# Layer 2 scan steps of two channel-and-state groups over half a chunk, with two PSUM places for the scan's inputs and two products ahead of two scans

One core of one Trainium2 chip. The metric is the device time of the whole program, in microseconds (us), of the slowest (here the only) core.

## The reference

Four layers on a 2 x 64 x 96 x 96 image: attention, a Mamba block, a bidirectional Mamba over rows and then columns, and a depthwise filter. The change touches layer 2. Cut to what matters there:

```python
def step(h, inp):                      # one position t of one sequence
    dt_t, B_t, C_t, x_t = inp
    dA = jnp.exp(dt_t[:, :, None] * A)                       # the decay
    h = dA * h + dt_t[:, :, None] * B_t[:, None, :] * x_t[:, :, None]
    return (h, jnp.einsum('nds,ns->nd', h, C_t))
...
y = jnp.swapaxes(ys, 0, 1) + x * p['Dp']
y = y * jax.nn.silu(z)
```

Sequences are 96 long and start from zero in layer 2. Layer 1 has the same step, but one sequence of 9216 per image, so there the state is carried from chunk to chunk.

## The kernel before

A unit is one chunk of 768 positions (8 sequences) in one direction. The 128 channels times 16 states are 2048 rows, taken as 16 groups of 128, one group a step: partition p holds state p // 8, and in step n channel (p + 8n) mod 128. (The prediction calls them channel groups.) For each step a read brings 128 rows of `dt` and `dt*x`, from row 8n on, from a copy in DRAM that holds every row twice; ScalarE turns `dt` into decays, VectorE (DVE) multiplies `dt*x` by `B` into PSUM and scans, GpSimd (POOL) multiplies by `C`, and TensorE (PE) gathers: it puts every row back to its channel and adds it into `y`, so that after 16 steps the states are summed.

```python
def read(self, u, step):
    u.dtu[step] = self.work("spread", 2 * CH, bufs=7)
    self.nc.sync.dma_start(out=u.dtu[step], in_=u.rows[8 * step : 8 * step + P])

def decay(self, u, step):
    da = u.dtu[step][:, :CH]
    self.nc.scalar.activation(da, da, AF.Exp, scale=u.w.rates[:, step : step + 1])

def scan(self, u, step):
    da, x = u.dtu[step][:, :CH], u.dtu[step][:, CH:]
    _, bx = self.two(self.ps_x, "x", "bx")          # one PSUM place, 2 x 512 columns
    nc.vector.tensor_mul(bx, x, u.B)                # u.B: 2 x 512 columns
    h = u.h[step] = self.work("h", bufs=7)
    ...
    nc.vector.tensor_tensor_scan(h[:, way], da[:, way], bx[:, way], first, ALU.mult, ALU.add)
    ...
    nc.gpsimd.tensor_mul(h, h, u.C)

def gather(self, u, step):                          # two matmuls, halves of the chunk
    ...
    self.nc.tensor.matmul(p, lhsT=self.t.gather[step], rhs=u.h[step][:, bass.ts(j, HALF)], ...)

# per unit, at fixed steps: (offset from the unit's first step, piece)
PIECES = (... (-25, "gate_mm"), (-23, "gate_read"),        # ScalarE: copy, table load, Silu, table load
          (-21, "step_mm"), (-19, "step_read"), (-18, "step_exp"), (-17, "step_kept"), ...
          (-9, "step_u"), (-8, "step_write"),              # GpSimd makes the rows, SyncE writes them
          (18, "y_read"), ...)                             # ScalarE drains y from PSUM
```

In the timelines shown here each engine's instructions stand in program order. That order for a step is: read of step n+5, decay of step n+3, product and scan of step n, gather of step n-2, then the pieces of that step.

## Time and profile before

| | before |
|---|---|
| time, median (range) of the 3 runs known then | 8538.82 us (8531.84 to 8540.03) |
| layer 1, first scan to first scan of layer 2 | 1188 us, 384 steps |
| layer 2, first 384 steps | 1170 us, 3.05 us each |
| layer 2, other 1152 steps (the quiet part) | 3346 us, 2.91 us each |

The stretches are taken from the starts of the scans in the trace. In the first part of layer 2 the weights of later blocks are still prepared between the steps. The lines on which the argument rests are in the prediction, with how to read them.

### The profile page before, as it was taken

The numbers are of one execution on the slowest core, as the hardware profiler recorded it, in microseconds if no ns is written. First come the engines' busy times: TensorE is split into PE (matmuls) and PEld (weight loads), VectorE is DVE, ScalarE is ACT, GpSimd is POOL, SyncE is SP. The second block draws the span as 40 slices with busy tenths as digits, with TensorE's granted clock in tenths as the row PEclk, the third lists the DMA queues.
The fourth block names the chain that finished last, engine by engine and source line by source line (L and its number), as shares of the span: only waits on it lengthen the run. The fifth ranks groups of instructions, "written<-read, shape, count | busy, mean of one in ns | idle before, by whom it ended". The sixth has DMA issues, their size and how long they took to land.

```text
span 8543.3 us, 77007 instructions
## 1 busy us (share of the span) xinstructions
PE 7689.6 (90%) x24578; PEld 3325.3 (39%) x24578; DVE 7074.4 (83%) x5136; ACT 4738.5 (55%) x4817; POOL 4786.7 (56%) x3146
## 2 busy tenths in 40 slices
PE   9999999999998999998898888888888888888887
PEld 3333333333333444444444444444444444444443
DVE  6666666666664999988888999999999999999998
ACT  4444444444444665665556566665655655565562
POOL 0000000000001888888777888888888888888884
PEclk9999999999997998888889999999999999999999
DMA  1000000000002877777777888888888888888884
GB/s 40 1 1 1 1 1 1 4 4 4 4 4 80 299 288 278 295 277 281 283 289 284 292 312 304 305 310 299 310 305 303 308 297 310 301 305 305 300 313 182
DMA packets 317287, 1725.61 MB, mean 202 GB/s; under 512 B 35268, under 2 KB 36420, under 8 KB 316360
## 3 DMA queue, kind: packets, MB, share of 16 engines
q1 hardware_dynamic: 315424, 1717.56, 54.7%
q8 instruction: 195, 3.19, 0.2%
q10 hardware_dynamic: 1448, 3.05, 0.1%
q14 instruction: 220, 1.80, 0.1%
HBM read 1522.68 MB, written 197.79 MB: 201 GB/s over the span
## 4 chain that ended last, share of the span: by engine, by line
DVE 33%; POOL 11%; PE 8%; DMA 8%; issue 5%; ACT 3%; DVEq 1%; SPq 0%; POOLq 0%; ACTq 0%
DVE h L842 21%; DVE bx L838 11%; POOL h L845 8%; DMA spread<-rows 6%; PE y_ssm L854 3%; PE mm L661 2%; DMA rows<-dtu 2%; PE conv L745 1%; ACT spread L826 1%; PE B L832 1%; POOL dtu L802 1%; POOL state L844 1%; PE conv L739 1%; DVE xa L1167 1%; DVEq L842 1%
## 5 line engine op out<-in xcount | busy, mean ns | idle before, releaser
L845 POOL TENSOR_TENSOR h<-h,C 128x768 f32<-128x768 f32 x1920 | 3484.1, 1815 | 818.2 <-DVE h L842 767.0
L854 PE MATMUL y_ssm<-h,pair 128*128 128x384 f32 x7680 | 2958.7, 522 | 324.9 <-POOL h L845 322.3
L842 DVE TENSOR_TENSOR_SCAN h<-spread,bx 128x768 f32<-128x768 f32 x1536 | 2694.4, 1754 | 228.5 <-ACT spread L826 20.4
L854 PEld LDWEIGHTS y_ssm<-h,pair 128*128 128x128 f32 x7680 | 1445.9, 198 | 1748.7 <-POOL h L845 670.2
L838 DVE TENSOR_TENSOR bx<-spread,B 128x768 f32<-128x768 f32 x1920 | 1846.5, 962 | 239.0 <-PE B L832 172.6
L363 DVE TENSOR_TENSOR acc_e<-acc_e,e 128x1536 f32<-128x1536 f32 x792 | 1390.0, 1755 | 684.4 <-ACT e L307 645.2
L826 ACT ACTIVATE spread<-spread,xa 128x768 f32<-128x768 f32 x1536 | 1405.1, 930 | 989.1 <-DMA spread<-rows 956.4
L307 ACT ACTIVATE e<-f_exp 128x1536 f32<-128x1536 f32 x864 | 1207.1, 1449 | 1223.7 <-PE f_exp L297 1223.7
L336 POOL TENSOR_TENSOR xa<-xa,t_att 64x512 f32<-64x512 f32 x36 | 45.5, 1263 | 2612.7 <-ACT t_att L334 2612.7
L314 PE MATMUL y_att<-e,xb 128*64 128x512 f32 x5184 | 1243.6, 601 | 0.0
L297 PE MATMUL f_exp<-theta,phi 64*128 64x512 f32 x5184 | 1234.4, 606 | 1.0 <-DVE xb L280 0.5
L297 PEld LDWEIGHTS f_exp<-theta,phi 64*128 64x128 f32 x5184 | 466.2, 186 | 754.6 <-issue 460.8
L842 DVE TENSOR_TENSOR_SCAN h<-spread,state,bx 128x768 f32<-128x768 f32 x384 | 696.0, 1813 | 66.9 <-ACT spread L826 15.7
L314 PEld LDWEIGHTS y_att<-e,xb 128*64 128x64 f32 x5184 | 341.5, 136 | 830.7 <-issue 829.3
L745 PE MATMUL conv<-xn,xa 64*128 64x384 f32 (+3 forms) x1536 | 595.5, 531 | 51.4 <-DVE xa L589 19.5
L756 ACT ACTIVATE raw<-conv,cols 128x768 f32<-128x768 f32 x120 | 108.2, 901 | 878.6 <-PE conv L745 632.6
L826 ACT ACTIVATE spread<-spread,rates 128x768 f32<-128x768 f32 x384 | 351.0, 930 | 148.6 <-DMA spread<-rows 146.1
L745 PEld LDWEIGHTS conv<-xn,xa 64*128 64x128 f32 x1536 | 291.8, 200 | 341.9 <-issue 139.0
L661 PE MATMUL mm<-raw,xa 128*128 128x384 f32 x768 | 287.4, 497 | 65.7 <-ACT xb L893 64.7
L832 PE MATMUL B<-raw,xa 128*128 128x384 f32 x384 | 181.2, 603 | 171.4 <-DVE bx L838 171.4
L792 POOL TENSOR_TENSOR kept<-dtu,kept 128x768 f32<-128x768 f32 x120 | 218.3, 1820 | 64.4 <-ACT kept L785 64.3
L739 PE MATMUL conv<-xn,taps 64*128 64x384 f32 x384 | 193.5, 662 | 37.8 <-DVE xa L589 18.9
(200 smaller groups left out, 5530.5 us busy)
## 6 DMA issues: line engine op xcount, KB each, us to landing
spread<-rows SPq DMA_DIRECT2D x1920, 768.0 KB, 5.3
rows<-dtu SPq DMA_DIRECT2D x240, 768.0 KB, 5.8
image<-pre SPq DMA_DIRECT2D x11, 384.0 KB, 2.3
xb<-image SPq DMA_DIRECT2D x11, 384.0 KB, 7.1
xa<-in_x SPq DMA_DIRECT2D x1, 2304.0 KB, 21.5
out<-xa ACTq DMA_DIRECT2D x7, 240.0 KB, 2.0
out<-xa SPq DMA_DIRECT2D x1, 1200.0 KB
xa<-in_x SPq DMA_DIRECT2D x3, 384.0 KB, 11.5
```

What stands on the lines that cost most here:

```text
L297: nc.tensor.matmul(fs[j // 3][:, bass.ts(j % 3, NB)], lhsT=phi[at, bass.ts(m // 2, P)], rhs=theta[at, bass.ts(i, NB)], start=True, stop=True,)
L307: nc.scalar.activation(e, f, AF.Exp)
L314: nc.tensor.matmul(y[rows_of(m % 2)], lhsT=g[:, m, :], rhs=es[j // 3][:, bass.ts(j % 3, NB)], start=m < 2, stop=m >= KEYS - 2,)
L363: nc.vector.tensor_add(acc, acc, e)
L661: self.nc.tensor.matmul(o, lhsT=lhsT, rhs=x, start=n == 0, stop=n == len(terms) - 1)
L739: self.nc.tensor.matmul(p, lhsT=lhsT, rhs=x[:, c0 - j : c0 + HALF - j], **flags)
L745: self.nc.tensor.matmul(p3[:, :, o], lhsT=lhsT, rhs=x3[:, :, i], **flags)
L826: self.nc.scalar.activation(da, da, AF.Exp, scale=u.w.rates[:, step : step + 1])
L838: nc.vector.tensor_mul(bx, x, u.B)
L842: nc.vector.tensor_tensor_scan(h[:, way], da[:, way], bx[:, way], first, ALU.mult, ALU.add)
L845: nc.gpsimd.tensor_mul(h, h, u.C)
L854: self.nc.tensor.matmul(p, lhsT=self.t.gather[step], rhs=u.h[step][:, bass.ts(j, HALF)], start=False, stop=step == self.STEPS - 1,)
```

## The change

Its intent: VectorE should not wait for its own last instruction. The scan depended on the product just ahead of it, and the next product had to write the PSUM place that the scan had just read. With a second place, and the order product, product, scan, scan, neither is so. To make room for the second place `B` and `y` shrink: in layer 2 a step becomes two groups over half a chunk (still 768 columns), with `B` and `y` of half a chunk in a tile of NB = 512 columns each. Both kernels allocate 8 x 512 columns of PSUM in these layers; that no more would fit was the premise. Decays go straight into the tile in which the scan runs in place. The core of the diff (layer 1's branch and set-up cut):

```diff
+        self.places = [self.wide(ps.tile([P, 2 * NB], FP, name=f"place{i}")) for i in range(2)]
+        self.low = [ps.tile([P, NB], FP, name=f"low{i}")[:, :HALF] for i in range(2)]
...
     def read(self, u, step):
-        u.dtu[step] = self.work("spread", 2 * CH, bufs=7)
-        self.nc.sync.dma_start(out=u.dtu[step], in_=u.rows[8 * step : 8 * step + P])
+        u.dtu[step] = self.work("spread", 2 * CH, bufs=6)
+        half, groups = self.paired(step)
+        for q, n in enumerate(groups):
+            row = u.rows[8 * n : 8 * n + P, bass.ts(half, CH)]
+            self.nc.sync.dma_start(out=u.dtu[step][:, bass.ts(q, CH)], in_=row)
     def decay(self, u, step):
-        da = u.dtu[step][:, :CH]
-        self.nc.scalar.activation(da, da, AF.Exp, scale=u.w.rates[:, step : step + 1])
+        h = u.h[step] = self.work("h", bufs=9)
+        for q, n in enumerate(self.paired(step)[1]):
+            dt = u.dtu[step][:, q * CH : q * CH + HALF]
+            self.nc.scalar.activation(h[:, bass.ts(q, HALF)], dt, AF.Exp, scale=u.w.rates[:, n : n + 1])
+    def inputs(self, u, step):
+        bx = self.places[step % 2][1].rearrange("p (q t) -> p q t", q=2)
+        x = u.dtu[step].rearrange("p (q a t) -> p q a t", q=2, a=2)[:, :, 1]
+        B = self.low[0].unsqueeze(1).to_broadcast([P, 2, HALF])
+        self.nc.vector.tensor_mul(bx, x, B)
     def scan(self, u, step):
+        bx = self.places[step % 2][1]
+        nc.vector.tensor_tensor_scan(h[:, way], h[:, way], bx[:, way], 0.0, ALU.mult, ALU.add)
+        C = u.C[:, bass.ts(self.paired(step)[0], HALF)]
+        nc.gpsimd.tensor_mul(h, h, C.unsqueeze(1).to_broadcast([P, 2, HALF]))
+    def y_half(self, u):                    # new piece at step 10: first half of y out of its tile
+        u.y = self.work("yg")
+        self.nc.scalar.copy(u.y[:, :HALF], self.low[1])
...  # in the loop over steps s of a unit
-                self.scan(*at(n))
-            if s == self.STEPS - 1 and at(n + 1):
-                self.shared(at(n + 1)[0])
+                elif s % 2 == 0:
+                    self.inputs(u, s)
+                    self.inputs(u, s + 1)
+                self.scan(u, s)
+                if u.paired and s == 6:
+                    self.shared(u, 1)       # B of the second half
+                if s == (14 if u.paired else 15) and unit(n // self.STEPS + 1):
+                    self.shared(after)      # B of the next unit's first half
```

More of the change, by code (lines that the diff above doesn't have):

```diff
@@ L630, with __init__ @@
     DECAY = 3
-    def __init__(self, k, tables, wk, dram, ps_b, ps_x, ps_y, ps_m):
+    def __init__(self, k, tables, wk, dram, ps, ps_m):
         self.k, self.nc, self.t = k, k.nc, tables
-        self.wk, self.dram, self.ps_b, self.ps_x, self.ps_y, self.ps_m = wk, dram, ps_b, ps_x, ps_y, ps_m
+        self.wk, self.dram, self.ps_m = wk, dram, ps_m
+        self.places = [self.wide(ps.tile([P, 2 * NB], FP, name=f"place{i}")) for i in range(2)]
+        self.low = [ps.tile([P, NB], FP, name=f"low{i}")[:, :HALF] for i in range(2)]
     def work(self, tag, n=CH, **kw):
@@ L639, in two, with wide @@
     @staticmethod
-    def two(pool, tag, name):
-        p = pool.tile([P, 2 * NB], FP, tag=tag, name=name)
+    def wide(p):
         return [p[:, NB - HALF : NB], p[:, NB : NB + HALF]], p[:, NB - HALF : NB + HALF]
@@ L650, in open @@
     def open(self, name="mm"):
-        return self.two(self.ps_m, "m", name)
+        return self.wide(self.ps_m.tile([P, 2 * NB], FP, tag="m", name=name))
     def half(self, sides, j, terms, rows=slice(0, P)):
@@ L671, in halves, with by_half @@
         return lambda j: t[:, bass.ts(j, HALF)]
+    @staticmethod
+    def by_half(t):
+        return t.rearrange("p (j t) -> p j t", j=2)
     def norm_centre(self, u):
@@ L775, in step_read @@
         u.both = self.work("dtu", 2 * CH, bufs=1)
-        u.dt, u.e = u.both[:, :CH], u.both[:, CH:]
-        u.kept = self.work("kept", bufs=1)
-        nc.scalar.activation(u.e, u.p, AF.Abs, bias=u.w.dt_b)
-        nc.scalar.activation(u.dt, u.p, AF.Relu, bias=u.w.dt_b)
+        order = "p (j a t) -> p a j t" if u.paired else "p (a j t) -> p a j t"
+        both = u.both.rearrange(order, a=2, j=2)
+        u.dt, u.e = both[:, 0], both[:, 1]
+        u.kept = self.by_half(self.work("kept", bufs=1))
+        p = self.by_half(u.p)
+        nc.scalar.activation(u.e, p, AF.Abs, bias=u.w.dt_b)
+        nc.scalar.activation(u.dt, p, AF.Relu, bias=u.w.dt_b)
     def step_exp(self, u):
@@ L787, in step_log @@
     def step_log(self, u):
-        u.log = self.work("log", bufs=1)
+        u.log = self.by_half(self.work("log", bufs=1))
         self.nc.scalar.activation(u.log, u.e, AF.Ln, bias=1.0)
@@ L801, in step_u @@
         nc = self.nc
-        nc.gpsimd.tensor_mul(u.e, u.dt, u.xc)
+        nc.gpsimd.tensor_mul(u.e, u.dt, self.by_half(u.xc))
         if not u.carry:
             first = W - 1 if u.rev else 0
-            nc.gpsimd.memset(u.dt.rearrange("p (n t) -> p n t", t=W)[:, :, first : first + 1], 1e30)
+            nc.gpsimd.memset(u.dt.rearrange("p j (n t) -> p j n t", t=W)[:, :, :, first : first + 1], 1e30)
     def step_write(self, u):
@@ L818, in c_read, with paired @@
         self.nc.scalar.copy(u.C, u.p)
+    def paired(self, step):
+        half, m = divmod(step, self.STEPS // 2)
+        return half, (2 * m, 2 * m + 1)
     def read(self, u, step):
-        u.dtu[step] = self.work("spread", 2 * CH, bufs=7)
-        self.nc.sync.dma_start(out=u.dtu[step], in_=u.rows[8 * step : 8 * step + P])
-    def decay(self, u, step):
-        da = u.dtu[step][:, :CH]
-        self.nc.scalar.activation(da, da, AF.Exp, scale=u.w.rates[:, step : step + 1])
-    def shared(self, u):
-        sides, u.B = self.two(self.ps_b, "b", "B")
-        for j, p in enumerate(sides):
-            self.nc.tensor.matmul(p, lhsT=u.w.bc[0], rhs=u.xc[:, bass.ts(j, HALF)], start=True, stop=True)
+        u.dtu[step] = self.work("spread", 2 * CH, bufs=6)
+        if not u.paired:
+            self.nc.sync.dma_start(out=u.dtu[step], in_=u.rows[8 * step : 8 * step + P])
+            return
+        half, groups = self.paired(step)
+        for q, n in enumerate(groups):
+            row = u.rows[8 * n : 8 * n + P, bass.ts(half, CH)]
+            self.nc.sync.dma_start(out=u.dtu[step][:, bass.ts(q, CH)], in_=row)
@@ new lines, in decay, with shared @@
+    def decay(self, u, step):
+        h = u.h[step] = self.work("h", bufs=9)
+        if not u.paired:
+            self.nc.scalar.activation(h, u.dtu[step][:, :CH], AF.Exp, scale=u.w.rates[:, step : step + 1])
+            return
+        for q, n in enumerate(self.paired(step)[1]):
+            dt = u.dtu[step][:, q * CH : q * CH + HALF]
+            self.nc.scalar.activation(h[:, bass.ts(q, HALF)], dt, AF.Exp, scale=u.w.rates[:, n : n + 1])
+    def shared(self, u, half=0):
+        if u.paired:
+            sides, halves = [self.low[0]], [half]
+        else:
+            (sides, u.B), halves = self.places[1], range(2)
+        for j, p in zip(halves, sides):
+            self.nc.tensor.matmul(p, lhsT=u.w.bc[0], rhs=u.xc[:, bass.ts(j, HALF)], start=True, stop=True)
@@ L834, in scan @@
+    def inputs(self, u, step):
+        if not u.paired:
+            u.bx = self.places[0][1]
+            self.nc.vector.tensor_mul(u.bx, u.dtu[step][:, CH:], u.B)
+            return
+        bx = self.places[step % 2][1].rearrange("p (q t) -> p q t", q=2)
+        x = u.dtu[step].rearrange("p (q a t) -> p q a t", q=2, a=2)[:, :, 1]
+        B = self.low[0].unsqueeze(1).to_broadcast([P, 2, HALF])
+        self.nc.vector.tensor_mul(bx, x, B)
     def scan(self, u, step):
         nc = self.nc
-        da, x = u.dtu[step][:, :CH], u.dtu[step][:, CH:]
@@ L837, in scan @@
-        _, bx = self.two(self.ps_x, "x", "bx")
-        nc.vector.tensor_mul(bx, x, u.B)
-        h = u.h[step] = self.work("h", bufs=7)
-        way = slice(None, None, -1) if u.rev else slice(None)
-        first = u.carry[:, step : step + 1] if u.carry else 0.0
-        nc.vector.tensor_tensor_scan(h[:, way], da[:, way], bx[:, way], first, ALU.mult, ALU.add)
-        if u.carry:
-            nc.gpsimd.tensor_copy(first, h[:, CH - 1 :])
-        nc.gpsimd.tensor_mul(h, h, u.C)
-    def gather(self, u, step):
-        if step == 0:
-            u.y_sides, u.y_all = self.two(self.ps_y, "y", "y_ssm")
-            for j, p in enumerate(u.y_sides):
-                self.nc.tensor.matmul(p, lhsT=u.w.direct, rhs=u.xc[:, bass.ts(j, HALF)], start=True, stop=False)
-        for j, p in enumerate(u.y_sides):
-            self.nc.tensor.matmul(
-                p,
-                lhsT=self.t.gather[step],
-                rhs=u.h[step][:, bass.ts(j, HALF)],
-                start=False,
-                stop=step == self.STEPS - 1,
-            )
@@ L862, in y_read @@
-    def y_read(self, u):
-        u.y = self.work("yg")
-        self.nc.scalar.copy(u.y, u.y_all)
+        h = u.h[step]
+        if not u.paired:
+            first = u.carry[:, step : step + 1]
+            nc.vector.tensor_tensor_scan(h, h, u.bx, first, ALU.mult, ALU.add)
+            nc.gpsimd.tensor_copy(first, h[:, CH - 1 :])
+            nc.gpsimd.tensor_mul(h, h, u.C)
+            return
+        bx = self.places[step % 2][1]
+        way = slice(None, None, -1) if u.rev else slice(None)
@@ new lines, in scan @@
+        nc.vector.tensor_tensor_scan(h[:, way], h[:, way], bx[:, way], 0.0, ALU.mult, ALU.add)
+        h = h.rearrange("p (q t) -> p q t", q=2)
+        C = u.C[:, bass.ts(self.paired(step)[0], HALF)]
+        nc.gpsimd.tensor_mul(h, h, C.unsqueeze(1).to_broadcast([P, 2, HALF]))
+    def gather(self, u, step):
+        if u.paired:
+            half, groups = self.paired(step)
+            parts = [(half, self.low[1], q, n) for q, n in enumerate(groups)]
+            begin, end = step % 8 == 0, step % 8 == 7
+        else:
+            parts = [(j, p, j, step) for j, p in enumerate(self.low)]
+            begin, end = step == 0, step == self.STEPS - 1
+        h = u.h[step]
+        if begin:
+            for half, p in {half: p for half, p, _, _ in parts}.items():
+                self.nc.tensor.matmul(p, lhsT=u.w.direct, rhs=u.xc[:, bass.ts(half, HALF)], start=True, stop=False)
+        for i, (_, p, q, n) in enumerate(parts):
+            stop = end and (i == 1 or not u.paired)
+            self.nc.tensor.matmul(p, lhsT=self.t.gather[n], rhs=h[:, bass.ts(q, HALF)], start=False, stop=stop)
@@ L866, in y_gate @@
+    def y_half(self, u):
+        if u.paired:
+            u.y = self.work("yg")
+            self.nc.scalar.copy(u.y[:, :HALF], self.low[1])
+    def y_read(self, u):
+        if u.paired:
+            self.nc.scalar.copy(u.y[:, HALF:], self.low[1])
+        elif not u.drained:
+            u.y = self.work("yg")
+            for j, p in enumerate(self.low):
+                self.nc.scalar.copy(u.y[:, bass.ts(j, HALF)], p)
     def y_gate(self, u):
@@ L920 @@
         (-8, "step_write"),
+        (10, "y_half"),
         (18, "y_read"),
@@ L927, with lates @@
     OTHER = (3, 5)
+    @staticmethod
+    def lates(now, s):
+        halves = now and now[0].paired
+        if s == 2 or (s == 10 and halves):
+            return ()
+        if s == 3 or (s == 11 and halves):
+            return (3, 2)
+        return (2,)
     def run(self, units, first, n_first, other):
         for u in units:
-            u.dtu, u.h = {}, {}
+            u.dtu, u.h, u.paired, u.drained = {}, {}, not u.carry, False
         steps = [(u, s) for u in units for s in range(self.STEPS)]
@@ L938, in run @@
         table = [[] for _ in range(self.STEPS)]
+        unit = lambda i: units[i] if i < len(units) else None
         for offset, name in self.PIECES:
@@ L961, in run @@
             if at(n):
-                self.scan(*at(n))
-            if s == self.STEPS - 1 and at(n + 1):
-                self.shared(at(n + 1)[0])
-            for late in {2: (), 3: (3, 2)}.get(s, (2,)):
-                if at(n - late):
+                u = at(n)[0]
+                if not u.paired:
+                    self.inputs(u, s)
+                elif s % 2 == 0:
+                    self.inputs(u, s)
+                    self.inputs(u, s + 1)
[3 more added lines that the diff above has]
+                if s == (14 if u.paired else 15) and unit(n // self.STEPS + 1):
+                    after = unit(n // self.STEPS + 1)
+                    if after.paired and not u.paired:
+                        for late in (2, 1, 0):
+                            self.gather(u, s - late)
+                        self.y_read(u)
+                        u.drained = True
+                    self.shared(after)
+            if n == -1:
+                self.shared(units[0])
+            for late in self.lates(at(n), s):
+                if at(n - late) and not (at(n - late)[0].drained):
                     self.gather(*at(n - late))
@@ L1002, in layers1_2 @@
         tc.tile_pool(name="ssm_d", bufs=2, space=bass.MemoryType.DRAM),
-        tc.tile_pool(name="ssm_b", bufs=1, space=PSUM),
         tc.tile_pool(name="ssm_x", bufs=1, space=PSUM),
-        tc.tile_pool(name="ssm_y", bufs=1, space=PSUM),
         tc.tile_pool(name="ssm_m", bufs=1, space=PSUM),
@@ L1018, in first @@
         def first(c):
-            ps, tag = ((m.ps_b, "b"), (m.ps_y, "y"), (m.ps_x, "x"))[c % 3]
-            pre.pointwise(k.xb[:, bass.ts(c, CH)], *m.two(ps, tag, "pc"))
+            pre.pointwise(k.xb[:, bass.ts(c, CH)], *(m.places[c % 3] if c % 3 < 2 else m.open()))
         carver = Carver(k.xa)
```

## The prediction

> **What bounds the kernel now.** I read the costliest groups of the page first, then the windows, then the chain of waits and the timeline of VectorE inside layer 2, then the list of waits. Layers 1 and 2 make 1920 scan steps, 384 in layer 1 and 1536 in layer 2. Each step is a product `bx` and a scan on VectorE (DVE), a product with `C` on GpSimd (POOL), one `Exp` on ScalarE (ACT), two gather matmuls (four instructions in the trace) and one 768 KB read.
>
> ```profile
> L845 POOL TENSOR_TENSOR h<-h,C 128x768 f32<-128x768 f32 x1920 | 3484.1, 1815 | 818.2 <-DVE h L842 767.0
> L842 DVE TENSOR_TENSOR_SCAN h<-spread,bx 128x768 f32<-128x768 f32 x1536 | 2694.4, 1754 | 228.5 <-ACT spread L826 20.4
> L838 DVE TENSOR_TENSOR bx<-spread,B 128x768 f32<-128x768 f32 x1920 | 1846.5, 962 | 239.0 <-PE B L832 172.6
> L826 ACT ACTIVATE spread<-spread,xa 128x768 f32<-128x768 f32 x1536 | 1405.1, 930 | 989.1 <-DMA spread<-rows 956.4
> ...
> 5600.00:6600.00 1000.00, 860.12 (x2319) 413.82 (x2318) 934.10 (x689) 612.58 (x674) 832.39 (x484) 0.97 0.83 306
> ```
>
> The reader is to see two things. DVE needs 1.754 + 0.962 = 2.716 us a step. In the quiet part of layer 2 (last line: busy PE, PEld, DVE, ACT, POOL, then clock, DMA share, GB/s) DVE is the busiest at 93%, and 345 scans begin there, 2.90 us a step. POOL waits mainly for the scan, ACT mainly for the DMA; neither sets the end. The chain says what the missing 7% is:
>
> ```profile
> 6004.37 0.97 DVE bx L838
> 6005.34 0.03 issue
> 6005.37 0.05 DVEq L842
> 6005.42 0.04 issue
> 6005.46 1.76 DVE h L842
> ```
>
> Product, 133 ns of nothing, scan, 34 ns (from the starts and ends in the trace), product. In the 133 ns the scan's semaphore wait is only answered when the product just before it has ended, and then the scan is issued. The median step is 2.883 us = 2.716 + 0.133 + 0.034. What DVE does when the next instruction is independent of the one in flight shows where weights of a later block are prepared between two steps:
>
> ```profile
> 4456.80 1.75 DVE L842 TENSOR_TENSOR_SCAN h<-spread,bx 128x768 f32<-128x768 f32 x1
> 4458.47 0.26 DVE L589 TENSOR_TENSOR xa<-mats,mm 128x128 f32<-128x128 f32 x1
> 4458.65 0.96 DVE L838 TENSOR_TENSOR bx<-spread,B 128x768 f32<-128x768 f32 x1
> 4459.74 1.75 DVE L842 TENSOR_TENSOR_SCAN h<-spread,bx 128x768 f32<-128x768 f32 x1
> ```
>
> 4456.80 + 1.75 is 4458.55, yet the next one starts at 4458.47; the product then starts at 4458.65, before 4458.73. In the trace such pairs overlap by 81 to 86 ns, in all 16 of the cases of this kind behind a scan, also where the second one waits for an older value of DVE's own semaphore.
>
> [...] 84 ns of overlap where nothing is waited for. [...] Product and scan have one input in PSUM; scans last 1753 to 1755 ns and POOL's products 1797 to 1830 ns in the window above[...]. [...] the trace has half-clock stretches of 3.4 us, two for each pair of units, where PE sits before `B`.
>
> **The change part by part.** In layer 2 a step becomes two channel groups over half the chunk, still 768 columns. The order of instructions on DVE is now product, product, scan, scan. Every one depends only on things at least two instructions back, so I expect all four joints of a pair of steps to overlap by 84 ns: (2 x 1.754 + 2 x 0.962 - 4 x 0.084) / 2 = **2.548 us** a step, against 2.883. That is 0.335 us x 1536 = 515 us if nothing else came to bind.
>
> Beside it, and not on DVE:
> - ACT makes two `Exp` of 384 columns instead of one of 768. From 830 ns for 768 and 1484 ns for 1536 columns a column costs 0.85 ns, so one of 384 is an estimated 0.60 us, two with ACT's own 0.1 us of overlap 1.1 us instead of 0.93. ACT goes from 28.1 to some 32 us a unit (16 steps).
> - Reads double in number at half the size. In the trace a 3072-byte packet took 121 ns (median) and a 6144-byte one 234, so the same bytes cost 3% more. The demand becomes 306 x 2.90 / 2.6 = 341 GB/s; over 12 us stretches the trace reached 424.
> - Decays go into the states' tiles (9 of them), so a read's buffer is free after the product and not after the scan; that pays for having 6 and not 7.
> - PE has as many matmuls as before, 108 a unit. At the 0.322 us between starts back to back this is 35 us, 38 us with the pauses at changes of weights. `B` is made twice a unit, and `y` is drained twice, with two more waits of PE.
> - Layer 1 keeps its dependent order: 384 steps, no change expected.
>
> **What binds instead.** A unit takes 46.6 us now. Floors after: DVE 16 x 2.548 = 40.8 us; POOL 38.7 us (its busy time without overlaps, per unit); PE about 38 us plus one or two waits of 2 us for a product before `B`; DMA 35 us (306 x 46.6 is 14.3 MB a unit, at 424 GB/s, and 3%). Nothing passes DVE, but POOL would be at 95% and PE at 93%, in queues in order, so some of the gain must come back as waits. The one I trust most:
>
> ```profile
> SPq L822 <- DVE h L842: 614.5, 257, 3.6
> SPq L811 <- POOL dtu L806: 141.0, 22, 6.7
> ...
> PEld B L832 <- DVE bx L838: 57.0, 22, 3.9
> PE B L832 <- DVE bx L838: 42.5, 22, 3.3
> ```
>
> The rows of the next unit are written when POOL has made them, once in each of 22 units, and SyncE stood 6.4 us for it. In one unit the write was issued 19.65 us before the next unit's first product, and that unit's first two reads landed 13.3 and 15.2 us after the write. At 2.55 us a step there are only some 16 us left. It should just fit; 2 us more of POOL's lag and each unit begins with a wait. I put 1.5 us a unit for all such waits: 42.3 us, **2.64 us** a step.
>
> The sum, from the starts of the scans: the last 1152 steps of layer 2 take 3346 us now (2.905 each) and 1152 x 2.64 = 3041 after: 305 saved. The first 384 take 1170 us (3.05 each), since weights are prepared between them and the clock is 0.81 to 0.93; PE is nearer its limit there, so I give half of the gain, 0.18 us x 384 = 69. 8539 - 374 = 8165, said as **8170 us**.
>
> **Rivals.**
> 1. Only the wait goes, not the overlap: joints of 34 ns as from scan to product now. Then 2.716 + 0.034 = 2.75 us a step, 0.133 less, at most 200 us: about 8340. For it: products wait on DVE's semaphore today and all show 34 ns. Against: there they wait for the instruction just ahead.
> 2. POOL becomes the bound. Its `h` times `C` now reads `C` twice through a repeated pattern of 2 x 384. A POOL product of 64 x 768 took 1.54 us flat and 1.81 us in 8 rows of 96, or 34 ns a row; two rows would add 0.03 to 0.07 us, 1 us a unit, still under DVE. At 0.2 us each POOL would need 42 us, 2.62 us a step plus waits: about 8230.
> 3. PE or the reads bind. With PE's clock at 0.85, as in the first part of layer 2, its 38 us become 43 to 45 us, 2.75 us a step: about 8330. Two small reads a step could also lower the DMA rate: the packets' own time is 0.83 of the engines' already, 40 us a unit with the 3%, and should they not gain by queueing, 330 GB/s is 2.69 us a step. Against: PE's idle times, which go with the half clock, should shrink.
> 4. The full 2.55 with hardly a wait: about 8050.
>
> **Range and chances.** I give the central course half, rival 1 and 3 together a quarter, rival 2 and 4 the rest: 8020 to 8340. Two per cent is 171 us, a step of about 2.79 us; rivals 1 and 3 together, or a new wait of 3 us at each unit, would be needed to miss it: faster 0.9, same 0.08, slower 0.02. A real slowdown needs the DMA to fall below 300 GB/s.
>
> **What would show it.** Right: scans still 1754 and products 962 ns, starts overlapping by 84 ns in the timeline, DVE above 95% busy, POOL near 92%, a median step near 2.55 and a mean near 2.64, layer 1 unchanged. Wrong: joints of 34 ns (rival 1); POOL's products above 1.95 us with DVE waiting on buffers (2); DVE waiting for `B`, or for `Exp` that wait for reads (3). The prediction fails most simply if the strided product or the scan in place is slower than 962 and 1754 ns: 0.1 us there costs 150 us.

## The result, and the profile after

| | before | after |
|---|---|---|
| time, median (range), 4 runs each | 8537.23 us (8531.84 to 8540.03) | 8177.18 us (8154.16 to 8195.08) |
| ratio of fast runs, 95% interval | | 0.9577 (0.9553 to 0.9602) |
| layer 1 | 1188 us | 1191 us |
| layer 2, first 384 steps | 1170 us, 3.05 each | 1071 us, 2.79 each |
| layer 2, other 1152 steps | 3346 us, 2.91 each | 3077 us, 2.67 each |

A ratio is the mean time of one kernel's fast runs over that of the other's of the same rounds, so not quite the ratio of the medians. The result is right in value. Of the 368 us between the two profiled runs 99 come from the first part of layer 2 and 269 from the rest.

From the costliest groups of the kernel after, and its busy times in a window of the quiet part:

```profile
L893 POOL TENSOR_TENSOR h<-h,C 128x768 f32<-128x768 f32 x1536 | 2755.1, 1819 | 231.7 <-DVE h L890 225.1
L890 DVE TENSOR_TENSOR_SCAN h<-h,place 128x768 f32<-128x768 f32 x1536 | 2604.3, 1737 | 4.9 <-ACT h L857 4.9
...
L857 ACT ACTIVATE h<-spread,xa 128x384 f32<-128x384 f32 x3072 | 1717.2, 607 | 368.7 <-DMA spread<-rows 336.8
L877 DVE TENSOR_TENSOR place<-spread,low 128x768 f32<-128x768 f32 x1536 | 1388.3, 949 | 251.0 <-PE low L866 238.4
...
5400.00:6400.00 1000.00, 910.84 (x2524) 464.43 (x2523) 942.98 (x750) 737.65 (x1131) 901.29 (x527) 0.96 0.89 333
```

VectorE's idle time before scans fell from 228 us to 5, and 375 steps begin in 1000 us, not 345. The product now waits for `B`, 238 us in all. VectorE's timeline, where one line of `x2` is two instructions back to back:

```profile
6024.27 3.39 DVE L890 TENSOR_TENSOR_SCAN h<-h,place 128x768 f32<-128x768 f32 x2
6027.58 1.80 DVE L877 TENSOR_TENSOR place<-spread,low 128x768 f32<-128x768 f32 x2
6029.29 3.39 DVE L890 TENSOR_TENSOR_SCAN h<-h,place 128x768 f32<-128x768 f32 x2
...
6034.30 3.39 DVE L890 TENSOR_TENSOR_SCAN h<-h,place 128x768 f32<-128x768 f32 x2
6040.18 1.83 DVE L877 TENSOR_TENSOR place<-spread,low 128x768 f32<-128x768 f32 x2 [2.49 <-PE low L866]
```

6027.58 lies before 6024.27 + 3.39: every joint overlaps. Between 6024.27 and 6029.29 are 5.02 us for two steps, 2.51 us a step. At 6040.18 a unit begins, and VectorE had waited 2.49 us for `B`. Who waited for whom in the same window of the quiet part (us in total, times, longest):

```profile
POOL kept L805 <- ACT kept L798: 56.0, 24, 4.3
DVE place L877 <- PE low L866: 53.5, 24, 4.1
...
PE low L907 <- ACT yg L915: 44.4, 12, 3.7
POOL h L893 <- DVE h L890: 40.8, 37, 2.1
...
DVE place L877 <- DMA spread<-rows: 3.4, 7, 1.0
```

In 23.4 units VectorE lost 53.5 us to `B` (2.3 us a unit) and only 3.4 to the reads. From the starts and ends in the trace, averaged over the quiet part, 1.74 us a unit stand before the first product and 0.64 before the ninth, where the second half's `B` is needed. Why `B` was late at 6040.18 is seen on ScalarE and then on PE:

```profile
6023.72 1.28 ACT L773 ACT_TABLE_LOAD   x1
...
6027.81 1.12 ACT L857 ACTIVATE h<-spread,xa 128x384 f32<-128x384 f32 x2
6028.84 0.46 ACT L915 COPY yg<-low 128x384 f32<-128x384 f32 x1
```

```profile
6022.79 2.85 PE L910 MATMUL low<-h,pair 128*128 128x384 f32 x8
6029.34 1.65 PE L907 MATMUL low<-raw,xa 128*128 128x384 f32 x2 [3.70 <-ACT yg L915]
6030.78 4.85 PE L910 MATMUL low<-h,pair 128*128 128x384 f32 x8
...
6036.76 2.74 PE L910 MATMUL low<-h,pair 128*128 128x384 f32 x8
6039.34 0.81 PE L866 MATMUL low<-raw,xa 128*128 128x384 f32 x2
```

PE had gathered the first half of `y` by 6025.6 and stood until ScalarE, busy with the Silu (1.49 us) and its two table loads (1.28 us each), drained it at 6028.84. PE's clock was at half for 6.83 us from 6028.19 on: eight gathers took 4.85 us and not 2.7. `B` (L866) stands behind all of them in PE's queue and came at 6040.15. The whole quiet part bears this out: PE stood over 2 us for the mid-unit drain in every second unit only, and the first product of the next unit then waited 3.04 us for `B` on average, against 0.44 us in the other units.

### The profile page after: what moved, and what is told of

Its sections match the earlier page's. It is cut to its first block, busy times and chain, and to the rows that moved or that the text cites.

```text
span 8174.9 us, 80364 instructions
## 1 busy us (share of the span) xinstructions
PE 7554.5 (92%) x24578; PEld 3358.0 (41%) x24578; DVE 6785.6 (83%) x5136; ACT 5045.4 (62%) x6473; POOL 4755.1 (58%) x3146
## 3 DMA queue, kind: packets, MB, share of 16 engines
q10 hardware_dynamic: 1448, 3.05, 0.1%
## 4 chain that ended last, share of the span: by engine, by line
PE 21%; POOL 13%; issue 12%; ACT 8%; DMA 8%; DVE 4%; SPq 0%; DVEq 0%; ACTq 0%; POOLq 0%
PE low L910 10%; DMA spread<-rows 6%; POOL h L886 5%; POOL h L893 4%; PE mm L666 4%; ACT h L857 4%; PE conv L754 4%; DVE place L877 2%; DMA rows<-dtu 1%; PE low L907 1%; PE conv L748 1%; DVE h L890 1%; POOL dtu L811 1%; PE low L866 1%; ACT raw L773 1%
## 5 line engine op out<-in xcount | busy, mean ns | idle before, releaser
L910 PE MATMUL low<-h,pair 128*128 128x384 f32 x7680 | 2865.4, 515 | 44.2 <-POOL h L886 26.5
L893 POOL TENSOR_TENSOR h<-h,C 128x768 f32<-128x768 f32 x1536 | 2755.1, 1819 | 231.7 <-DVE h L890 225.1
L890 DVE TENSOR_TENSOR_SCAN h<-h,place 128x768 f32<-128x768 f32 x1536 | 2604.3, 1737 | 4.9 <-ACT h L857 4.9
L910 PEld LDWEIGHTS low<-h,pair 128*128 128x128 f32 x7680 | 1503.2, 201 | 1288.6 <-issue 270.7
L857 ACT ACTIVATE h<-spread,xa 128x384 f32<-128x384 f32 x3072 | 1717.2, 607 | 368.7 <-DMA spread<-rows 336.8
L877 DVE TENSOR_TENSOR place<-spread,low 128x768 f32<-128x768 f32 x1536 | 1388.3, 949 | 251.0 <-PE low L866 238.4
L884 DVE TENSOR_TENSOR_SCAN h<-h,state,place 128x768 f32<-128x768 f32 x384 | 696.1, 1813 | 67.7 <-ACT h L853 19.2
L754 PE MATMUL conv<-xn,xa 64*128 64x384 f32 (+3 forms) x1536 | 557.9, 503 | 16.6 <-DVE xa L1128 5.3
L872 DVE TENSOR_TENSOR place<-spread,place 128x768 f32<-128x768 f32 x384 | 369.1, 961 | 129.3 <-PE place L866 116.9
L853 ACT ACTIVATE h<-spread,rates 128x768 f32<-128x768 f32 x384 | 351.1, 931 | 175.0 <-DMA spread<-rows 173.6
L907 PE MATMUL low<-raw,xa 128*128 128x384 f32 x384 | 220.2, 662 | 257.8 <-ACT yg L915 175.6
L805 POOL TENSOR_TENSOR kept<-dtu,kept 128x768 f32<-128x768 f32 x120 | 218.2, 1819 | 285.1 <-ACT kept L798 285.1
```

The costliest lines, as they stand in the source:

```text
L754: self.nc.tensor.matmul(p3[:, :, o], lhsT=lhsT, rhs=x3[:, :, i], **flags)
L857: self.nc.scalar.activation(h[:, bass.ts(q, HALF)], dt, AF.Exp, scale=u.w.rates[:, n : n + 1])
L877: self.nc.vector.tensor_mul(bx, x, B)
L884: nc.vector.tensor_tensor_scan(h, h, u.bx, first, ALU.mult, ALU.add)
L890: nc.vector.tensor_tensor_scan(h[:, way], h[:, way], bx[:, way], 0.0, ALU.mult, ALU.add)
L893: nc.gpsimd.tensor_mul(h, h, C.unsqueeze(1).to_broadcast([P, 2, HALF]))
```

## The experiments

Kernels ran, each with three rounds beside the kernel before. Kernels called wrong stayed within the comparison's tolerance, but they are no versions to use. "Quiet part" is the mean step of the last 1152 steps, in the one profiled run of each. How far such stretches can be trusted shows in layer 1, which the first six edits to the changed kernel (the rows from dependent to one_exp) leave alone: in the change and these six runs it took 1176 to 1191 us.

| run | what it does | median us | ratio (95%) | quiet part |
|---|---|---|---|---|
| decays_only | before, decays in the states' tiles | 8517.23 | 0.9969 (0.9948 to 0.9990) | 2.89 |
| dependent | after, order P S P S | 8420.86 | 0.9858 (0.9832 to 0.9884) | 2.79 |
| one_ahead | after, one product ahead | 8236.98 | 0.9619 (0.9598 to 0.9639) | 2.70 |
| (the change) | two ahead of two | 8177.18 | 0.9577 (0.9553 to 0.9602) | 2.67 |
| b_first | B ahead of two gathers | 8158.11 | 0.9531 (0.9506 to 0.9556) | 2.67 |
| no_mid_drain | wrong: no drain in mid-unit | 8119.41 | 0.9499 (0.9483 to 0.9515) | 2.64 |
| half_gathers | wrong: 30% fewer matmuls | 8063.99 | 0.9445 (0.9423 to 0.9467) | 2.60 |
| one_exp | wrong: one Exp a step | 8131.22 | 0.9518 (0.9499 to 0.9537) | 2.65 |
| kept_later | a GpSimd piece one step later | 8226.95 | 0.9634 (0.9613 to 0.9654) | 2.72 |
| write_later | the write behind two reads | 8125.69 | 0.9515 (0.9490 to 0.9539) | 2.60 |
| b_first_write | b_first and write_later | 8062.38 | 0.9431 (0.9411 to 0.9452) | 2.59 |
| b_both_write | the same, B early in both halves | 8126.90 | 0.9505 (0.9479 to 0.9531) | 2.59 |
| b_both_write_y | the same, drain ahead of the Silu | 8431.17 | 0.9868 (0.9846 to 0.9889) | 2.81 |

### Where the gain comes from

**dependent**

```diff
-                elif s % 2 == 0:
-                    self.inputs(u, s)
-                    self.inputs(u, s + 1)
+                else:
+                    self.inputs(u, s)      # B at s == 7 and 15, not 6 and 14
```

> Undoes only the order: product, scan, product, scan, with the half-chunk layout and both PSUM places kept. Theory (the gain is the overlap of independent neighbours on VectorE): each scan again follows its own product at 133 ns, the next product follows the scan at minus 84 ns because its place is the other one. Step 1.754 + 0.949 + 0.133 - 0.084 = 2.75 us against 2.51 median of the changed kernel, about 0.24 x 1536 = 370 us more if the waits for B stayed, some 100 less because a slower VectorE waits less: 8400 to 8560 us, ratio to before 0.985 to 1.0. Rival (the gain comes from the layout, the smaller B or the earlier release of the reads' buffers): it stays near 8180 us, ratio 0.96.

VectorE's timeline of it:

```profile
6000.09 0.94 DVE L877 TENSOR_TENSOR place<-spread,low 128x768 f32<-128x768 f32 x1
6001.16 1.75 DVE L890 TENSOR_TENSOR_SCAN h<-h,place 128x768 f32<-128x768 f32 x1
6002.83 0.94 DVE L877 TENSOR_TENSOR place<-spread,low 128x768 f32<-128x768 f32 x1
```

The scan starts 0.13 us after the product ends, the product 0.08 us before the scan ends: a median step of 2.742 us, as expected. The half-chunk layout, the smaller `B` and the second place together give 1.4%; of the 0.141 us by which the median step is shorter, 0.118 lie at the joint from scan to product (34 ns before, 84 ns of overlap here) and 0.020 in the shorter product. The order gives the other 2.8%.

**one_ahead**

```diff
+                else:
+                    if s % 8 == 0:
+                        self.inputs(u, s)
+                    if s % 8 != 7:
+                        self.inputs(u, s + 1)
```

> One product ahead of one scan with the two places (product of the next step, then this scan). Theory: the scan no longer depends on its neighbour (minus 91 ns), but the product after it writes the place that this scan has just read, so this joint stays at about 34 ns: 1.74 + 0.95 - 0.09 + 0.03 = 2.63 us median against 2.51, 0.12 x 1536 = 190 us if nothing else moved, some less since the waits shrink: 8270 to 8370 us. Rival (only the read after write counts, not the write after read): median step 2.51 and 8180 us.

```profile
6000.85 0.96 DVE L877 TENSOR_TENSOR place<-spread,low 128x768 f32<-128x768 f32 x1
6001.72 1.75 DVE L890 TENSOR_TENSOR_SCAN h<-h,place 128x768 f32<-128x768 f32 x1
6003.50 0.96 DVE L877 TENSOR_TENSOR place<-spread,low 128x768 f32<-128x768 f32 x1
```

The other way round: the scan overlaps, and the product, which overwrites what the scan has just read, starts 34 ns after it. A median step of 2.653 us. So a write after a read counts as a neighbour's wait too, and that is what the second product ahead removes. The time, 8237, is below what I expected: the change's own quiet part is only 0.03 us a step better, though its chain is 0.145 us shorter. That is the sign of a second bound near 2.67.

**decays_only**

```diff
-        da = u.dtu[step][:, :CH]
-        self.nc.scalar.activation(da, da, AF.Exp, scale=u.w.rates[:, step : step + 1])
+        h = u.h[step] = self.work("h", bufs=9)
+        self.nc.scalar.activation(h, u.dtu[step][:, :CH], AF.Exp, scale=u.w.rates[:, step : step + 1])
...  # cut: 6 and not 7 buffers for reads, the scan in place
```

> The kernel before with only the decays put into the states' tiles (6 buffers for reads, 9 for states), no half chunks, no new order. Both theories of the order: VectorE's chain of 2.883 us a step is untouched, 8520 to 8560 us, ratio 0.997 to 1.003, and scans still 1754 ns. Rival (the earlier release of buffers or the scan in place gives part of the gain, also the 17 ns by which scans became shorter): 8440 to 8500 us and scans of 1737 ns.

```profile
L842 DVE TENSOR_TENSOR_SCAN h<-h,bx 128x768 f32<-128x768 f32 x348 | 610.4, 1754 | 42.9 <-DVE bx L838 1.9
```

The gain is 0.3%. The scan in place takes 1754 ns, the median step is 2.883 us as before. The chain was not quite untouched: in 543 of 1142 joints of the quiet part the scan started some 104 ns after its product and not 133, about 16 us in all; why is not known. So the 17 ns by which scans are shorter in the change are not from the place they write; they go with the overlap (1754 here and in "dependent", 1744 in "one_ahead", 1737 with both neighbours independent).

### What eats the rest

**no_mid_drain** (wrong)

```diff
     def y_half(self, u):
             u.y = self.work("yg")
-            self.nc.scalar.copy(u.y[:, :HALF], self.low[1])
     def y_read(self, u):
+            self.nc.scalar.copy(u.y[:, :HALF], self.low[1])
             self.nc.scalar.copy(u.y[:, HALF:], self.low[1])
```

> Wrong on purpose: the first half of y is not drained in the middle of the unit (both halves are copied at its end), so TensorE has nothing to wait for there. Theory (what is left of VectorE's idle time, 2.5 us a unit before the first or ninth product, comes from B being late behind the drain that sits behind the gate's Silu on ScalarE): the waits of the product for B fall from 2.3 to under 0.7 us a unit, worth 96 x 1.7 = 160 us: 7980 to 8060 us. Rival (B is late because GpSimd or the reads are late, or because TensorE has too much work): over 8130 us and the same waits.

```profile
PE low L907 <- ACT yg L919: 63.4, 24, 5.6
...
DVE place L877 <- PE low L866: 49.5, 27, 3.2
```

Between the two theories: 60 us faster, but the waits for `B` stay, 49.5 us against 53.5. I had only moved the drain: PE now waits 63.4 us for the one at the end of the unit (18.9 in the change). By its total the run does not settle it, but by its places it speaks for the theory: PE's long pause moved to the other unit of each pair, and the long wait before a first product moved with it (2.16 us after a unit with the pause, none after the others; in the change 3.04 and 0.44).

**b_first**

```diff
+        if halves and s in (12, 13, 14):
+            return (4, 3, 2) if s == 14 else ()
```

> TensorE makes B of the next unit ahead of the gathers of steps 10 and 11 and not behind them. Theory (lateness of TensorE after the drain of y reaches VectorE through B alone): B comes some 2.6 us earlier in TensorE's queue, the wait before the first product of a unit falls from 1.7 to under 0.5 us, 96 x 1.2 = 115 us: 8040 to 8100 us. Rival (the delay passes through the gathers and the states' tiles, so that moving them back costs elsewhere): 8150 us or more, with new waits of the Exp for the gathers.

```profile
L877 DVE TENSOR_TENSOR place<-spread,low 128x768 f32<-128x768 f32 x374 | 339.6, 950 | 52.4 <-PE low L866 26.7 <-DMA spread<-rows 25.5
```

The wait before the first product fell from 1.74 to 0.22 us, as the theory said, and the time hardly moved: 0.5%, and next to nothing of it in the quiet part (2.67 us a step as before). It fell in the rival's range, but the rival's sign is absent (the Exp waited 1.5 us in the window for gathers, 4.0 in the change). What was saved came back mostly as a wait for the reads of steps 14 and 15 (1.09 us a unit against 0.15; 25.5 us in the window, 3.4 before), the rest before the ninth product (0.99 us against 0.64), so there is a second late thing behind the first.

**half_gathers** (wrong)

```diff
-            parts = [(half, self.low[1], q, n) for q, n in enumerate(groups)]
+            parts = [(half, self.low[1], q, n) for q, n in enumerate(groups)][:1]
```

> Wrong on purpose: of the two gather matmuls of a step only the first is made, 32 of TensorE's 108 instructions a unit fewer, all else the same. Theory (what is left of VectorE's idle time is TensorE late with B, because it idles for the drain, falls to half clock and then has too little slack to catch up): the waits of the product for B nearly vanish (under 0.5 us a unit), 2 us x 96 = 190 us: 7950 to 8030 us. Rival (another engine, GpSimd or the reads, sets about 42.5 us a unit and B is only where it shows): over 8110 us, with the waits moved to the reads or to the Exp.

```profile
L877 DVE TENSOR_TENSOR place<-spread,low 128x768 f32<-128x768 f32 x385 | 349.4, 949 | 31.6 <-DMA spread<-rows 17.1 <-PE low L866 14.2
```

With less work PE catches up, though it idles more and its mean clock falls to 0.907 (0.955 in the change): waits for `B` drop from 53.5 to 14.2 us, and the reads show again. 1.4% faster than the change. That `B` is late because PE has too little slack is thereby shown; so is the second wait. The time, 8064, lies between the ranges of theory and rival.

**one_exp** (wrong)

```diff
-        for q, n in enumerate(self.paired(step)[1]): ...two activations of 384
+        self.nc.scalar.activation(h, dt, AF.Exp, scale=u.w.rates[:, n : n + 1])   # 2 x 384, one rate
```

> Wrong on purpose: one Exp of 768 columns with the first group's rates in place of two of 384, as the kernel before has it. Measures what the added ScalarE instructions cost: 16 x some 0.2 us a unit of ScalarE's time. Theory (ScalarE only passes on the drain's lateness): B's wait shrinks by about a third, 8090 to 8150 us. Rival (ScalarE is the hidden bound since it was given two instructions for one): below 8050 us. Rival (ScalarE has slack enough): 8160 to 8190 us.

```profile
L878 DVE TENSOR_TENSOR place<-spread,low 128x768 f32<-128x768 f32 x380 | 343.9, 947 | 43.1 <-PE low L867 37.4 <-DMA spread<-rows 5.6
```

As the theory had it: 0.6%, with the waits for `B` down by a third. The second Exp of a step costs that much. That it acts through the drain is not shown: PE's wait for the mid-unit drain went only from 44.4 to 42.2 us in the window, that for the drain at the end of the unit from 18.9 to 12.1, and that for ScalarE's copy of `C` from 24.0 to 17.1.

**kept_later**

```diff
-        (-17, "step_kept"),
         (-17, "step_log"),
         (-17, "c_mm"),
+        (-16, "step_kept"),
```

> Right result: GpSimd's subtraction for the softplus is placed one step later, behind one more product with C, so that it no longer stands waiting for ScalarE (2.3 us a unit in the changed kernel). Theory (GpSimd, busy 38.7 us of 42.7, is a second pacemaker by being blocked at the head of its queue): its wait for ScalarE falls under 1 us a unit, 50 to 120 us gained: 8060 to 8130 us. Rival (GpSimd has slack, only TensorE's lateness counts): 8150 to 8200 us.

```profile
L893 POOL TENSOR_TENSOR h<-h,C 128x768 f32<-128x768 f32 x365 | 655.4, 1822 | 118.7 <-DVE h L890 113.4 <-PE mm L666 4.8
```

My theory fell. Its first half is right, the wait for ScalarE is gone; but GpSimd then waits 113 us for scans (41 in the change), and the kernel is 0.6% slower. GpSimd's wait for ScalarE is thus no loss by itself. What was lost is at the reads: SyncE stood 203.7 us in the window for the next unit's rows (178.0 in the change), and the product of step 15 waited 0.75 us a unit for its read (0.15 in the change), that of step 14 0.10. These waits make up nearly all of the 0.73 us by which a unit became longer.

**write_later**

```diff
-        (-8, "step_write"),
+        (-6, "step_write"),
```

> Right result: SyncE's command to write the rows of the next unit stands behind the reads of steps 14 and 15 and no longer ahead of them, where it blocks them for the 7.7 us in which GpSimd finishes the rows. Theory (the first wait that counts is that for B, the reads are the second and stand hidden behind it): the product of step 15 no longer waits (0.15 us a unit), B's wait stays near 2.4 us or grows, 8140 to 8185 us. Rival (the prediction's own: reads late at the head of a unit are what costs): under 8080 us.

```profile
PE low L907 <- ACT yg L915: 44.4, 12, 3.7
DVE place L877 <- PE low L866: 40.8, 20, 3.6
...
PE mm L666 <- ACT C L831: 19.0, 12, 2.6
```

Faster than my theory said, 0.6% below the change, and not by as much as the rival. The wait for the read of step 15 is gone and the wait of the ninth product too (0.01 us); the first product still waits 1.47 us. SyncE's queue had stood behind the write for 178 us in the window (23 times) with two reads behind it; now it stands 61.4 us. So the reads act on `B` without VectorE ever waiting long for them. The way that suggests itself is from late reads to the Exp, to the drain, to PE. The trace speaks against it: PE's wait for the mid-unit drain is the same 44.4 us, 12 times, in both runs (130 us over the quiet part in both). What became shorter is PE's wait for ScalarE's copy of `C` (78.8 to 50.9 us over the quiet part), and of PE's stretches at half clock, 55 and 38 in the quiet part, those behind that wait went from 19 to 3. No run tested either way by itself.

**b_first_write**: both of the last two edits.

> Both: B of the next unit ahead of two gathers, and the write behind two reads. Theory: with B early the wait for the reads of steps 14 and 15 (1.1 us a unit in the run with B first alone) was what ate the gain; now it goes as well, 1.1 us x 96 = 105 us below that run: 8030 to 8090 us. Rival (GpSimd or TensorE sets about 42.4 us a unit whatever the order): 8130 us or more, with the waits moved to the ninth product.

```profile
5400.00:6400.00 1000.00, 918.79 (x2576) 468.83 (x2575) 962.18 (x764) 733.94 (x1147) 916.20 (x537) 0.97 0.93 338
6400.00:7400.00 1000.00, 921.56 (x2641) 476.32 (x2640) 983.33 (x781) 740.57 (x1181) 937.56 (x551) 0.98 0.94 346
```

As expected, and the fastest version that computes the right thing: 0.9431 of the kernel before, about 1.5% below the change (0.9431 / 0.9577). VectorE is 96% and 98% busy. PE falls to half clock once in a pair of units (36 stretches in 36 pairs), and almost only behind the drain.

**b_both_write_y** and **b_both_write**. Both keep the write behind two reads (cut below) and put `B` ahead of two gathers in either half; the first also drains `y` before the Silu.

```diff
+        if halves and s in (4, 5, 6, 12, 13, 14):
+            return (4, 3, 2) if s in (6, 14) else ()
         (-23, "gate_read"),                # in b_both_write_y: the copy alone
+        (9, "y_half"),                     # only in b_both_write_y
+        (-23, "gate_silu"),                # only in b_both_write_y
```

> The same with B ahead of two gathers in both halves of the unit, and with the mid-unit drain of y placed on ScalarE before the Silu of the gate and its two table loads. Theory: TensorE idles less for the drain, so it keeps the full clock, the waits for B fall under 0.7 us a unit and those for the reads stay small: mean step 2.55 to 2.60 in the quiet part, 7940 to 8030 us. Rival (the drain put first makes ScalarE wait for the gathers and everything behind it late): not under 8080 us, with the scans waiting for the Exp.

> The last but one run without the moved drain: B ahead of two gathers in both halves, the write behind the reads of steps 14 and 15. Theory (the drain moved ahead of the Silu was the whole loss of the last run, by holding the Exp of step 13 back): the scans wait for no Exp again, the waits for B go from 1.05 us a unit to under 0.5, 7970 to 8050 us[...]. Rival (gathers moved back in the first half of the unit hold the states' tiles, and so the Exp): 8150 us or more with scans waiting for the Exp.

The window of b_both_write_y:

```profile
L892 DVE TENSOR_TENSOR_SCAN h<-h,place 128x768 f32<-128x768 f32 x356 | 606.0, 1738 | 105.0 <-ACT h L859 87.5 <-POOL h L895 17.4
```

No wait for `B` is left, yet it is slow, because ScalarE, standing for PE ahead of the drain (83 us in the window), gives the Exp of step 13 late: the scan of step 13 waits 4.7 us a unit. The rival was right. Without the moved drain most of that wait goes (0.43 us is left), as my theory for the last run said, but the time does not reach 8050: the first part of layer 2 takes 1105 us against 1041 in b_first_write, which stays unexplained, and the quiet part is the same to 3 us.

That last equality has a form. Before the last run I had expected that pairs of units of 85.33 us would become pairs of 81.92 us, and they did not. A pair of units (32 steps) takes 85.33 us, or 25.0 intervals of 3.413 us, in the quiet part's first third, and 81.92 us, 24.0 intervals, in most pairs after it, in both kernels, although their waits stand at different places. 3.413 us is the step in which the trace records PE's clock: in the change's trace 213 of its 214 stretches at full or half clock, all but the one at the end of the record, are a whole number of them. VectorE's own chain would allow 23.5 (32 x 2.508 us). In b_first_write the 24 pairs with one interval at half clock take 24.03 intervals on average, the 11 pairs with two take 24.97. That these pairs last whole intervals is shown; what closes the loop (PE's idle stretch behind the drain, the half clock after it, and the late work that this makes) is only argued, and no run took the clock away to prove it.

## Why the prediction was right

- **The total.** 8170 predicted, 8177 measured. That it is so close is luck, by misses that cancel: the quiet part was 0.03 us a step slower than said (2.67 against 2.64, 36 us over 1152 steps), the first part of layer 2 faster (2.79 against 2.87, 31 us). The gain there was to be only half because PE is nearer its limit; it was 0.26 us a step, no less than the 0.23 of the quiet part. (The 0.18 us put there is half of what the chain alone gives, 2.905 less 2.548, not half of the 0.265 put for the rest.) And within the quiet part the chain came out 0.6 us a unit shorter than said and the waits 1 us longer.
- **The overlap**, the main step: right. Measured 83 to 94 ns at all four joints. Rival 1 (34 ns) is refuted for independent neighbours, and "one_ahead" shows 34 ns exactly where the neighbour is not independent. The chain is 2.51 and not 2.548 us, mostly because scans and products that overlap also last 17 and 13 ns less, which I had not foreseen.
- **The wait that takes gain back**: the size was under, the place was wrong. The step that failed is "the one I trust most", the reads at the head of a unit. 1.5 us a unit was put for all waits. VectorE waited 2.5 us, of which 0.15 for reads; nearly all was for `B`, late behind the drain of `y`. DVE waiting for `B` was one of the signs that I had listed for being wrong (rival 3). I had listed "two more waits of PE" for `y` and `B`, but in the floors I counted only the waits for a product and not the one for ScalarE's drain. The reads do act, unseen on VectorE ("write_later").
- **ScalarE, reads, decays**: 607 ns an Exp against 0.60 estimated; 333 GB/s against 341; earlier release of buffers worth 0.3% at most. Right.
- **GpSimd** (rival 2): 1819 ns against 1815; the repeated pattern of `C` costs 4 ns and not 30 to 70. Refuted. It was 90% busy, not 92.
- **PE's half clock** (in rival 3): PE's idle time should shrink, and the half clock with it. The first came true (pauses over 60 ns: 499 us in the quiet part before, 291 after), the second did not: 54 stretches at half clock before, 55 after, a clock of 0.96 in the window (0.97 before). 35 of the 55 follow the wait for the mid-unit drain, which is new. My reading of the stretches before was off too: not two for each pair of units, but 54 in 36 pairs, and only 31 of them behind PE's pause before `B`, 22 behind gathers that waited for GpSimd. This is the part of rival 3 that held.
- **VectorE above 95% busy**: 94.3%, because of the longer waits for `B`; layer 1 unchanged (1188 and 1191 us): right.

## What to carry to other kernels

On a saturated engine whose instructions stand in program order, as in the timelines here, look at what each instruction waits for among its nearest neighbours, reads and overwrites alike: two independent chains taken in turn, two places each, removed 13% of VectorE's time per step here. Expect less than the chain gains (here 0.375 us of chain gave 0.23 us of step), because work that used to hide behind the bound engine then sets the pace; follow the new wait back through the queues, past the engine that it names, to the piece that stands at the head of one. A fix of one wait alone may show nothing while a second stands behind it: here two moves worth 0.5% and 0.6% alone gave 1.5% together.

## What the runs show of the engines

- VectorE, order: with the instructions the same in number and kind, order alone moved the median step from 2.742 ("dependent") to 2.653 ("one_ahead") to 2.508 us (the change). In these traces independent neighbours overlap by 83 to 94 ns (the change), a product that overwrites what the scan just ahead has read starts 34 ns after it (the kernel before, "one_ahead"), and a scan that reads what the product just ahead wrote 129 to 133 ns after it (in half the joints of "decays_only" 104).
- VectorE, durations: an overlapped instruction is also recorded shorter in these traces, scans 1737 ns in the change against 1754 in the kernel before, products 942 ("dependent") to 949 (the change) against 962.
- TensorE's clock: in the change PE stood 3.70 us up to 6029.34, and the clock was at half for 6.83 us from 6028.19 on. Pairs of units took 24.0 or 25.0 times 3.413 us (81.92 and 85.33 us) for most of the quiet part in two kernels, b_first_write and b_both_write; the cause is not shown.
- GpSimd, a repeated operand: a product reading `C` as 2 x 384 twice took 1819 ns in the change, against 1815 flat in the kernel before.
